# Two interleaved recurrences on one core: half of the second one's input product is issued behind the first one's reset product

## The chip, the cores and the metric

The kernel runs on one core of one Trainium2 chip. The metric is the device time of one execution in microseconds; of the kernel before there are three timed runs and one profiled execution. All arithmetic of the part that matters here is in float32.

## The reference, cut to what matters

The input `x` is 32 rows of 256 steps with 256 features, and four layers are added to it one after the other. The first is a GRU, the second a leaky gated recurrence over the result, the third is computed with cumulative sums over time, and the fourth is a two-matrix network whose weights are made per row from `cond_1024`.

```python
# layer 0, for t = 0 .. 255, h starts at zero
z = sigmoid(x_t @ W_z + h @ U_z + vz)
r = sigmoid(x_t @ W_r + h @ U_r + vr)
hh = tanh(x_t @ W + (r * h) @ U + vh)
h = (1 - z) * h + z * hh
# layer 1 on x1 = x + (all h), for the same t, h1 starts at cond_1024
gate = sigmoid(h1 @ Wh.T + x1_t @ Wz.T + b)
h1 = tanh(h1 * (1 - alpha) + gate * x1_t)
# x2 = x1 + (all h1); then layers 2 and 3 on x2
```

So each of the 256 steps of the GRU depends on the one before. Layer 1 is a second recurrence that needs only step s of the first, and can run one step behind it.

## The kernel before, in words

**The state.** Feature dimensions of 256 are cut into NC = 2 chunks of 128, which is the depth of one pass through TensorE. The state of a step stands transposed, `hT` with 128 features by 32 rows in each chunk, so that it is the stationary operand of the products; the 256 outputs are cut into Q = 4 quarters of 64, one in each group of 32 PSUM partitions. One `product` is therefore a loop over two chunks and four quarters, which is eight matmuls in the source. The trace has sixteen pairs of weight load and matmul for each such product: every float32 matmul stands there twice.

**One turn of the loop** (`for t in range(T + 1)`) does step t of the first recurrence and step s = t - 1 of the second. TensorE's order in a turn is written out by hand (the loop stands in a `manual_schedule` block, so every engine executes in the order of the source):

1. `product(p_0[t], ..., hT, w_urz)`: reset and update gates from `hT`. ACT takes the sigmoid `r` in two halves (by_halves, L657), then the update gate `z` (L707), then the tanh of the second recurrence (`h1T`, L686).
2. `due(products, t)`: one product of side work, from a table of due times. In most turns it is half of a gate product for layer 2 (`pg`, L93), in others a product for the weights of layer 3 (`pw`, L429 and L489). Some early turns have none; four turns near the end have two.
3. `product(p_1[s], ..., pairs1[s], w_1z)`: the second recurrence's product of x + h. `pairs1` was added up by POOL (L750). Its last matmul also waits for `z_done`, the update gate of this turn (`after(done, z_done)`).
4. DVE forms `rh = r * h` in two halves (L725) and transposes each (`rhT`, L649); then `product(p_0[t], ..., rhT, w_uh)`, the reset product.
5. `product(p_1[s], ..., h1T, w_1h)`: the second recurrence's product of its state. After it ACT can take its sigmoid `gt` (L755).
6. ACT takes the tanh of the candidate in two halves (`other`, L657), DVE scans `h` (L639) and transposes it to `hT` (L649). Meanwhile TensorE does `project(t + 1)`, the product of the next x with `W_rzh`, 192 columns wide. In two of every four turns `project` first starts a new PSUM tile of the first recurrence with four bias matmuls of 384 columns (`begin("0", ...)`, L600).
7. Every eighth turn, a new PSUM tile of the second recurrence is started behind the projection with four bias matmuls of 512 columns (`begin_1`, L600). It waits for `gt`, as `p_1` has one buffer.
8. ACT scales `h1T` into `pairs1` (L757), then any side sigmoid that is due (`gate_f` and `gate_i`, L130). DVE transposes `gt` (L766) and scans `pre` (L639), from which ACT takes `h1T` in the next turn.

After the loop come layers 2 and 3 (from 735 us on), which the diff does not touch.

Of the kernel before, what the change touches and what calls it, by code (L numbers as in the profile page):

```python
# [19 lines left out]
NC = D // P  # L20
# [19 lines left out]
def kernel(ctx: ExitStack, tc: tile.TileContext, a, out: bass.AP):  # L40
# [23 lines left out]
    def flat(x):  # L64
        return x.rearrange("p c b -> p (c b)")
# [114 lines left out]
    with ExitStack() as rec:  # L180
# [27 lines left out]
        def load_wq(name, g):  # L208
            w, src = weights(name, g)
            nc.sync.dma_start(out=w, in_=src)  # L210
            return w
# [3 lines left out]
        def load_x(i):  # L215
            xTs[i] = xp.tile([P, NC, TB, B], FP, name=f"xT_{i}", tag="xT")
            nc.sync.dma_start(out=xTs[i], in_=a["xT"][:, i])
# [24 lines left out]
        with tc.manual_schedule():  # L242
# [30 lines left out]
            w_1z = load_wq("l1_Wz", 1)  # L273
# [291 lines left out]
        def due(when, t):  # L565
            return [f(*args) for f, args in when.get(t, ())]

        def product(ps, cols, hT, w):


            for k in range(NC):
                for j in range(Q):
                    last = nc.tensor.matmul(  # L573
                        ps[j * B : (j + 1) * B, cols],
                        hT[:, k, :],
                        w[:, k, j, :],
                        start=False,
                        stop=False,
                        skip_group_check=True,
                        tile_position=(0, j * B),  # L580
                    )
            return last

        def after(later, earlier):

            tc.add_manual_dep(
                later.ins,
                earlier.ins.name,
                mybir.DependencyInfo(mybir.DependencyClass.Sync, mybir.DependencyReason.DATA),
                reason="a wait taken early",  # L590
            )
# [21 lines left out]
        def cols_0(t, first, last):  # L613
            at = t // 2 % U0 * 3 * S
            return slice(at + first * S, at + (last + 1) * S)

        def cols_1(s):
            u = s if s < U1_0 else (s - U1_0) % U1
            return slice(u * S, (u + 1) * S)

        def step_tile(name):
            return sp.tile([P, NC, B], FP, name=name, tag=name)
# [9 lines left out]
        def pair_tile(name, bufs=3):  # L632
            return sp.tile([P, S, 2], FP, name=name, tag=name, bufs=bufs)
# [11 lines left out]
        def turned(name, src):  # L645

            dst = step_tile(name)
            for c in range(NC):
                nc.vector.transpose(dst[:, c], src[:, bass.ts(c, B)])  # L649
            return dst  # L650

        def by_chunk(x):
            return x.rearrange("p (c b) -> p c b", b=B)

        def by_halves(dst, src, function):
            for c in range(NC):
                nc.scalar.activation(dst[:, bass.ts(c, B)], src[:, bass.ts(c, B)], function)  # L657

        def x_of(t):
            return xTs[t // TB][:, :, t % TB, :]  # L660

        p_0, p_1, pairs1, h1s = {}, {}, {}, {}

        def project(t):
            if t // 2 % U0 == 0:
                ps = begin("0", slice(0, 3 * S), U0, t)
                for u in range(U0):
                    p_0[t + 2 * u] = ps
            return product(p_0[t], cols_0(t, 0, 2), x_of(t), w_x)

        def begin_1(s, steps):
            ps = begin("1", slice(3 * S, 4 * S), steps, s)
            for u in range(steps):
                p_1[s + u] = ps

        with tc.manual_schedule():
            h1T = condT
            project(0)
            late = None

            def finish_1():

                nonlocal h1T
                s, pre = late
                h1T = h1s[s] = step_tile("h1T")
                nc.scalar.activation(flat(h1T), pre, AF.Tanh)  # L686

            def residual(s):
                return nc.gpsimd.tensor_add(  # L689
                    X2[:, :, :, s], by_chunk(pairs1.pop(s)[:, :, 0]), h1s.pop(s)  # L690
                )

            for t in range(T + 1):
                s, run0, run1 = t - 1, t < T, t >= 1
                due(transfers, t)
                if run0 and t % TB == 0 and t // TB + 2 < NB:
                    load_x(t // TB + 2)
                if run0:
                    keep = pair_tile("keep")
                    z, kept = keep[:, :, 0], keep[:, :, 1]  # L700
                    if t > 0:
                        rz_done = product(p_0[t], cols_0(t, 0, 1), hT, w_urz)
                        r = sp.tile([P, S], FP, name="r", tag="r")
                        by_halves(r, p_0[t][:, cols_0(t, 0, 0)], AF.Sigmoid)
                    else:
                        nc.gpsimd.memset(kept, 0.0)
                    z_done = nc.scalar.activation(z, p_0[t][:, cols_0(t, 1, 1)], AF.Sigmoid)  # L707
                if late is not None:
                    finish_1()
                    late = None  # L710
                due(moves, t)
                due(products, t)
                if run1:
                    if s == 0:
                        begin_1(0, U1_0)
                    done = product(p_1[s], cols_1(s), by_chunk(pairs1[s][:, :, 0]), w_1z)
                    if run0:

                        after(done, z_done)
                rh_done = kept_done = None  # L720
                if run0 and t > 0:
                    rh = sp.tile([P, S], FP, name="rh", tag="rh")
                    for c in range(NC):
                        cs = bass.ts(c, B)
                        rh_done = nc.vector.tensor_mul(rh[:, cs], r[:, cs], h[:, cs])  # L725
                    rhT = turned("rhT", rh)
                    product(p_0[t], cols_0(t, 2, 2), rhT, w_uh)

                    kept_done = nc.vector.scalar_tensor_tensor(
                        kept, z, 1.0, h, ALU.subtract, ALU.mult, reverse0=True  # L730
                    )

                    after(kept_done, rz_done)
                if t >= 3:
                    done = residual(t - 3)
                    if rh_done is not None:
                        after(done, rh_done)
                for done in due(additions, t):
                    if done is not None:
                        after(done, kept_done)  # L740
                due(sums, t)
                if run1:
                    product(p_1[s], cols_1(s), h1T, w_1h)
                if run0:
                    other = others[t % 2]
                    by_halves(other[:, :, 1], p_0[t][:, cols_0(t, 2, 2)], AF.Tanh)
                    h = multiply_add("h", other, keep, NC)
                    hT = turned("hT", h)
                    pairs1[t] = pair_tile("pairs1", 6)
                    nc.gpsimd.tensor_add(by_chunk(pairs1[t][:, :, 0]), x_of(t), hT)  # L750
                    if t + 1 < T:
                        project(t + 1)
                if run1:
                    gt = sp.tile([P, S], FP, name="gt", tag="gt")
                    nc.scalar.activation(gt, p_1[s][:, cols_1(s)], AF.Sigmoid)  # L755
                    for c in range(NC):
                        nc.scalar.activation(  # L757
                            by_chunk(pairs1[s][:, :, 1])[:, c], h1T[:, c], AF.Copy,
                            scale=leak[:, c : c + 1],
                        )  # L760
                    if t % U1 == U1_0 and run0:

                        begin_1(t, min(U1, T - t))
                    due(sigmoids, t)
                    other = others[2 + t % 2]
                    nc.vector.transpose(other[:, :, 1], gt)  # L766
                    late = s, multiply_add("pre", other, pairs1[s])
            for t in sorted(t for t in transfers if t > T):
                due(transfers, t)
            finish_1()  # L770
            for s in (T - 2, T - 1):
                residual(s)
# [242 lines left out]
```

## Time and profile before

| | |
|---|---|
| median of three runs | 955.35 us (955.17 to 957.66) |
| the profiled execution's own time | 956.46 us |
| its span, first to last instruction | 954.6 us |
| mean granted TensorE clock | 0.995 |
| TensorE busy | 919.4 us, 96% of the span |
| VectorE (DVE) busy | 788.4 us, 83% |
| ScalarE (ACT) busy | 572.3 us, 60% |
| GpSimd (POOL) busy | 236.5 us, 25% |

The recurrences take the first 735 us or so of the span. In the views, PE is the matmul stream and PEld the weight loads. A row of the timeline gives the start and the length in microseconds, the engine, the line, what is written from what, the shape, the number of like instructions merged into the row, and in square brackets how long the engine sat idle before it and what released it. A row of the waits gives engine, line, what was waited for, the total in microseconds, the number of times and the longest. Lines with L573 are the matmuls of all products, so they are told apart by their tiles: `w_U_rz` (step 1), `w_l_Wz` (step 3), `w_U_h` (step 4), `w_l_Wh` (step 5), `w_W_rzh` (step 6). Ends of matmuls are modelled: a matmul of 64 columns is drawn 219 ns long although the next group starts 56 ns after it.

### The profile page before, as it was taken

The numbers are of one execution on the slowest core, as the hardware profiler recorded it, in microseconds if no ns is written. First come the engines' busy times: TensorE is split into PE (matmuls) and PEld (weight loads), VectorE is DVE, ScalarE is ACT, GpSimd is POOL, SyncE is SP. The second block draws the span as 40 slices with busy tenths as digits, with TensorE's granted clock in tenths as the row PEclk, the third lists the DMA queues.
The fourth block names the chain that finished last, engine by engine and source line by source line (L and its number), as shares of the span: only waits on it lengthen the run. The fifth ranks groups of instructions, "written<-read, shape, count | busy, mean of one in ns | idle before, by whom it ended". The sixth has DMA issues, their size and how long they took to land.

```text
span 954.6 us, 55121 instructions
## 1 busy us (share of the span) xinstructions
PE 919.4 (96%) x22806; PEld 630.6 (66%) x22806; DVE 788.4 (83%) x3409; ACT 572.3 (60%) x2648; POOL 236.5 (25%) x594
## 2 busy tenths in 40 slices
PE   7999999999999999999999999999998989999978
PEld 4666666666666666666666666666675557777756
DVE  5767788888888888888888888888776799999994
ACT  3455555555555555555555555555554788889972
POOL 1233322222222222222222222222222022222222
PEclk9999999999999999999999999999999999999989
DMA  8344212222222222222222222432241457777543
GB/s 265 108 126 147 79 51 92 65 73 92 70 92 77 92 66 67 91 70 90 69 86 76 65 97 66 131 119 83 73 128 54 122 165 230 224 228 224 188 158 117
DMA packets 104158, 107.71 MB, mean 113 GB/s; under 512 B 9153, under 2 KB 86241, under 8 KB 103906
## 3 DMA queue, kind: packets, MB, share of 16 engines
q1 hardware_dynamic: 103906, 104.18, 34.4%
q8 instruction: 179, 2.93, 1.3%
q14 instruction: 73, 0.60, 0.2%
HBM read 59.06 MB, written 45.09 MB: 109 GB/s over the span
## 4 chain that ended last, share of the span: by engine, by line
PE 80%; DVE 13%; ACT 3%; issue 2%; DMA 1%; POOL 0%; DVEq 0%; POOLq 0%; ACTq 0%
PE p L573 45%; PE ps_l L889 10%; PE pg L93 10%; PE ps_c L93 5%; DVE h L639 5%; PE p L600 3%; PE ps_g L93 2%; PE pw L489 2%; ACT other L657 2%; DVE hT L649 1%; ACT r L657 1%; DVE rh L725 1%; DVE cc L848 1%; DVE gate_g L138 1%; PE pw L429 1%
## 5 line engine op out<-in xcount | busy, mean ns | idle before, releaser
L573 PE MATMUL p<-w_W_rzh,xT 128*32 128x192 f32 x4096 | 214.8, 326 | 0.2 <-issue 0.2
L657 ACT ACTIVATE other<-p 128x32 f32<-128x32 f32 x512 | 74.2, 199 | 172.9 <-PE p L573 172.9
L639 DVE TENSOR_TENSOR_SCAN h<-other,keep 128x64 f32<-128x64 f32 x512 | 121.3, 278 | 66.3 <-ACT other L657 62.7
L573 PE MATMUL p<-w_U_rz,hT 128*32 128x128 f32 x4080 | 165.4, 279 | 6.0 <-DVE hT L649 0.2
L750 POOL TENSOR_TENSOR pairs<-xT,hT 128x64 f32<-128x64 f32 x256 | 82.2, 321 | 326.9 <-DVE other L766 273.6
L657 ACT ACTIVATE r<-p 128x32 f32<-128x32 f32 x510 | 72.8, 195 | 149.0 <-PE p L573 149.0
L689 POOL TENSOR_TENSOR X<-pairs,h1T 128x64 f32<-128x64 f32 x256 | 103.0, 402 | 214.9 <-DVE rhT L649 211.8
L573 PEld LDWEIGHTS p<-w_U_rz,hT 128*32 128x32 f32 x4080 | 97.4, 108 | 84.3 <-DVE hT L649 83.4
L639 DVE TENSOR_TENSOR_SCAN pre<-other,pairs 128x128 f32<-128x128 f32 x256 | 123.3, 481 | 34.2 <-ACT pairs L757 0.7
L573 PEld LDWEIGHTS p<-w_W_rzh,xT 128*32 128x32 f32 x4096 | 124.9, 110 | 22.4 <-issue 1.9
L573 PEld LDWEIGHTS p<-w_l_Wz,pairs 128*32 128x32 f32 x4096 | 79.2, 110 | 86.0 <-issue 69.2
L757 ACT ACTIVATE pairs<-h1T,leak 128x32 f32<-128x32 f32 x510 | 133.6, 314 | 0.4
L573 PE MATMUL p<-w_l_Wz,pairs 128*32 128x64 f32 x4096 | 120.3, 225 | 5.1 <-ACT keep L707 1.6
L573 PE MATMUL p<-w_U_h,rhT 128*32 128x64 f32 x4080 | 106.6, 221 | 0.4 <-issue 0.4
L573 PE MATMUL p<-w_l_Wh,h1T 128*32 128x64 f32 x4080 | 104.7, 219 | 0.8 <-issue 0.7
L725 DVE TENSOR_TENSOR rh<-r,h 128x32 f32<-128x32 f32 x510 | 74.9, 188 | 32.1 <-ACT r L657 5.7
L649 DVE STREAM_TRANSPOSE hT<-h 128x32 f32<-128x32 f32 x512 | 84.1, 198 | 0.0
L882 POOL TENSOR_TENSOR X<-X,w 128x512 f32<-128x512 f32 x32 | 41.4, 1306 | 165.3 <-DVE w L875 76.8
L649 DVE STREAM_TRANSPOSE rhT<-rh 128x32 f32<-128x32 f32 x510 | 80.0, 195 | 0.0
L573 PEld LDWEIGHTS p<-w_l_Wh,h1T 128*32 128x32 f32 x4080 | 76.4, 110 | 1.3 <-issue 1.0
L573 PEld LDWEIGHTS p<-w_U_h,rhT 128*32 128x32 f32 x4080 | 69.7, 108 | 5.5 <-issue 0.6
L686 ACT ACTIVATE h1T<-pre 128x64 f32<-128x64 f32 x256 | 69.5, 271 | 1.4 <-DVE pre L639 1.4
(108 smaller groups left out, 1470.5 us busy)
## 6 DMA issues: line engine op xcount, KB each, us to landing
adapted<-wm SPq DMA_DIRECT2D x128, 128.0 KB
wt<-adapted SPq DMA_DIRECT2D x28, 512.0 KB
xT<-in_xT_dram SPq DMA_DIRECT2D x32, 256.0 KB
w<-in_W_dram SPq DMA_DIRECT2D x32, 256.0 KB
out_dram<-y SPq DMA_DIRECT2D x32, 256.0 KB
gates<-gate_i SPq DMA_DIRECT2D x48, 128.0 KB
gates<-gate_s SPq DMA_DIRECT2D x48, 128.0 KB
gates<-gate_g SPq DMA_DIRECT2D x48, 128.0 KB
```

The source lines that it names most:

```text
L93: nc.tensor.matmul(ps[:, 0 : (h1 - h0) * (rows.stop - rows.start) * CT].rearrange("p (h b t) -> p h b t", h=h1 - h0, t=CT), w[:, k, e * P ...
L573: last = nc.tensor.matmul(ps[j * B : (j + 1) * B, cols], hT[:, k, :], w[:, k, j, :], start=False, stop=False, skip_group_check=True, tile_ ...
L639: nc.vector.tensor_tensor_scan(*(x[:, ns].rearrange("p n u -> p (n u)") for x in (done, other, pairs)), 0.0, ALU.mult, ALU.add,)
L649: nc.vector.transpose(dst[:, c], src[:, bass.ts(c, B)])
L657: nc.scalar.activation(dst[:, bass.ts(c, B)], src[:, bass.ts(c, B)], function)
L686: nc.scalar.activation(flat(h1T), pre, AF.Tanh)
L689: return nc.gpsimd.tensor_add(X2[:, :, :, s], by_chunk(pairs1.pop(s)[:, :, 0]), h1s.pop(s))
L725: rh_done = nc.vector.tensor_mul(rh[:, cs], r[:, cs], h[:, cs])
L750: nc.gpsimd.tensor_add(by_chunk(pairs1[t][:, :, 0]), x_of(t), hT)
L757: nc.scalar.activation(by_chunk(pairs1[s][:, :, 1])[:, c], h1T[:, c], AF.Copy, scale=leak[:, c : c + 1],)
L882: after(nc.gpsimd.tensor_add(x, x, ws[g][:, b]), on_vector)
L889: nc.tensor.matmul(ps[:, e, :], matrices[row][:, m, k, e * P : (e + 1) * P], src[:, k, :], start=(k == 0), stop=(k == NC - 1),)
```

## The change

`product` gets a list of chunks. The second recurrence's product of x + h (step 3) does only its first chunk where the whole stood, and its second chunk behind the reset product (step 4), ahead of the product of `h1T` (step 5). The wait for `z_done` is now on the last matmul of the first chunk. The number of instructions on every engine is the same, and no other engine's instructions move.

```diff
-        def product(ps, cols, hT, w):
+        def product(ps, cols, hT, w, chunks=range(NC)):
-            for k in range(NC):
+            for k in chunks:
                 for j in range(Q):
                     last = nc.tensor.matmul(
...
-                    done = product(p_1[s], cols_1(s), by_chunk(pairs1[s][:, :, 0]), w_1z)
+                    x_and_h = p_1[s], cols_1(s), by_chunk(pairs1[s][:, :, 0]), w_1z
+                    done = product(*x_and_h, [0])
                     if run0:
 
                         after(done, z_done)
...
                 if run1:
+
+                    product(*x_and_h, [1])
                     product(p_1[s], cols_1(s), h1T, w_1h)
```

## The prediction

> **What bounds the kernel now.** The page comes first, and it misleads:
>
> ```profile
> PE 919.4 (96%) x22806; PEld 630.6 (66%) x22806; DVE 788.4 (83%) x3409; ACT 572.3 (60%) x2648; POOL 236.5 (25%) x594
> PE 80%; DVE 13%; ACT 3%; issue 2%; DMA 1%; POOL 0%; DVEq 0%; POOLq 0%; ACTq 0%
> ```
>
> TensorE looks like the bound, in busy time and in the chain that ended last. But matmul ends are modelled: every product is drawn 0.15 to 0.35 us longer than the stretch after which the next can start. So I went on to the waits, where the weight loads show what TensorE stands for:
>
> ```profile
> ACT other L657 <- PE p L573: 172.9, 255, 1.3
> ACT r L657 <- PE p L573: 149.0, 255, 1.4
> PEld p L573 <- DVE hT L649: 83.4, 249, 0.6
> DVE h L639 <- ACT other L657: 62.7, 154, 1.2
> ```
>
> In 249 of 255 turns TensorE stands idle for `hT`. For `rhT` no wait is listed, which would say that TensorE itself is late at the reset product; that is what this change would cure. The timeline of one turn, in narrow windows, decides:
>
> ```profile
> 402.58 0.27 PEld L573 LDWEIGHTS p<-w_l_Wz,pairs 128*32 128x32 f32 x16 [0.33 <-issue]
> 402.55 0.21 DVE L649 STREAM_TRANSPOSE rhT<-rh 128x32 f32<-128x32 f32 x1
> 402.68 0.18 DVE L649 STREAM_TRANSPOSE rhT<-rh 128x32 f32<-128x32 f32 x1
> 402.81 0.27 PEld L573 LDWEIGHTS p<-w_U_h,rhT 128*32 128x32 f32 x16
> ...
> 403.94 0.18 DVE L649 STREAM_TRANSPOSE hT<-h 128x32 f32<-128x32 f32 x1
> 404.17 0.38 PEld L573 LDWEIGHTS p<-w_U_rz,hT 128*32 128x32 f32 x16 [0.26 <-DVE hT L649]
> ```
>
> The first half of `hT` ends at 404.12, the load that needs it starts at 404.17; the first half of `rhT` ends at 402.76, its load starts at 402.81. Read one instruction at a time, both hand-overs take 53 ns. Over the trace, the first load of the reset product comes 52 to 54 ns behind its transpose in 249 of 255 turns, that of its second chunk 52 to 54 ns behind the second transpose in 245. So both halves of the loop are latency chains: hT, gate product, `r`, `rh`, `rhT` (1.435 us) and reset product, tanh, scan, `hT` (1.364 us), together 2.80 us a turn. The product of x + h ends barely in time, but in time.
>
> **Taken from in front of the reset product.** Eight of sixteen matmuls leave. In a stream, groups of four 64-column matmuls start 56 ns apart (the product of `h1T`, 16 matmuls, takes 223 ns to the start of the next), so 112 ns leave. Worth:
> - Turns without side work already have this state: there the x + h product is all issued 235 ns before the reset product, and they last 2796 ns on average. Turns with a gate product last 2798.5, turns with four `pw` matmuls for layer 3 2806. If the difference is TensorE's lateness, it all goes: 172 x 2.5 = 0.43 us and 32 x 10 = 0.33 us.
> - Four late turns with two side products last 2885 ns; there the reset product comes 115 ns behind `rhT`. 4 x 88 = 0.35 us.
> - In two turns (5 and 250) TensorE is hundreds of ns late after a stall of its own: between 0 and 112 ns each, 0.11 us for both.
>
> In all 1.2 us, not the 255 x 0.112 = 28.6 us that the busy share promises. The ends are 0.35 us and 1.3 us.
>
> **Put behind the reset product.** The same eight matmuls, 112 ns, now stand ahead of the product of `h1T`, the projection, the bias matmuls and so the next gate product. No bank, wait or semaphore is added; the last reset matmul carries its own count in the built program, and the tanh waits for that. What is queued behind is where the cost must be looked for. In a turn without bias matmuls TensorE then stands idle (0.43 us before that `w_U_rz` row, 0.26 to 0.27 us in the others), but idle weight loads are not a margin of the matmul stream. The stretch from the start of the last group to the gate product is:
>
> ```profile
> 403.94 0.40 PE L600 MATMUL p<-parts,eye 128*32 128x512 bf16 x4
> 404.18 0.65 PE L573 MATMUL p<-w_U_rz,hT 128*32 128x128 f32 x16
> ...
> 406.08 0.35 PE L600 MATMUL p<-parts,eye 128*32 128x384 bf16 x4
> 406.73 0.35 PE L573 MATMUL p<-w_W_rzh,xT 128*32 128x192 f32 x4
> 406.98 0.65 PE L573 MATMUL p<-w_U_rz,hT 128*32 128x128 f32 x16
> ```
>
> - A group of the gate product follows another 109 ns later, but the first after an idle stretch 133 ns: 24 ns of slack that a late TensorE gets back.
> - Turns that start a tile of the first recurrence (406.08): the last projection group starts 243 ns before the gate product and occupies 162 ns (the spacing of such groups). Margin 243 - 162 + 24 = 105 ns against 112. 119 such turns are 7 to 8 ns late: 0.95 us.
> - Turns that start a tile of the second (403.94): the 512-column group starts 242 ns ahead. Its own length in a stream is not shown; the 384-column one occupies 163 ns, so 217 in proportion. Margin 242 - 217 + 24 = 49 ns, 62 ns late. 30 turns: 1.86 us. If it occupied only the 162 of the projection: 8 ns and 0.2 us; with twice 163, 5 us. I take proportion, since the float32 version of the same matmul, in the one turn where it streams, takes 428 ns, twice 214.
> - The other 96 turns have a margin above 0.26 us: nothing.
> - Six disturbed turns (2, 3, 4, 19, 31, 248) start the gate product as soon as TensorE can: 0 to 112 ns each; half, 0.34 us.
> - `gt` comes 112 ns later, and behind it ACT's two scalings, a side sigmoid and DVE's `pre`. Cover: the scalings end at 401.38, `pre` starts at 401.73 behind DVE's own transpose that ends at 401.59, so 0.16 us beyond the hand-over. A side sigmoid (406.88 for 0.46) ends 0.21 us before the gate product that reuses its bank (407.55). `begin_1` waits for `gt`, ends near 403.76 before and near 403.87 after, while the projection keeps TensorE until 404.05. Without cover it would be 112 ns a turn.
>
> A lateness here is not given back: the chain that follows has no slack.
>
> **Sum.** +1.86 + 0.95 + 0.34 - 0.43 - 0.33 - 0.35 - 0.11 = +1.9 us. Against the profiled execution (956.46 us: 954.6 span, 1.9 around it) that is 958.4; that execution lies 1.1 us above the median, so against the median of 955.35 I predict 957.3. About 0.3% (2.9 us) is what a measurement of this kernel can tell from no change; this is 0.2%.
>
> A rule of the Trainium skill would give another sign. By the page "TensorE: Matmul & The Clock Gate", section "Back-to-back issue gap", matmuls of 1 to 64 columns follow each other after some 60 cycles, an issue floor of about 25 ns. An estimate from it makes the moved piece, two rounds, 50 ns instead of 112: both margins would cover it but for a nanosecond or so, and the sum would be about -0.9 us. The rows of this trace say 56 ns a round for float32, so the measurement is taken.
>
> **The rivals.**
> - *The thin margin (slower).* 149 turns pay every nanosecond by which the moved stretch exceeds its margin. At 118 ns instead of 112, or with the 24 ns of start-up slack not given back in full (18), the sum passes +2.9 us and the change is measurably slower; at 130 ns it is +4.6, near 960.0. For it: no row of before shows a reset product followed by this one, and the margin is 7 ns wide of the mark already. Against: the stream's spacing of 56 ns stays the same from product to product. Chance 0.39.
> - *TensorE is late at the reset product after all (faster).* If the 53 ns were TensorE's and not the hand-over's, every turn would gain up to 112 ns, and the time fall to 927. Against: the same 53 ns stands at `hT`, where TensorE is idle. A smaller way: some 20 turns lose 6 us in all to stalls of TensorE that have no releaser ("issue"); half gone is -3, near 954. Chance 0.08 for both.
> - *The change doesn't do what it says:* the tanh waiting for the second chunk too would cost 255 x 0.112, near 984. The program's order and counts speak against it; 0.02, on the slower side.
>
> **How the numbers follow.** My forecast, within 0.3%, 0.51; slower 0.41; faster 0.08. Own range of the forecast: gains of 0.35 to 1.3 against costs of 1.15 (the short end for 512 columns, none for the disturbed turns) to 3.5 (all of those) give -0.15 to +3.1 us; the far end of 5 us for 512 columns is left out. The runs before spread over 2.5 us, and the thin margin is held up to 130 ns: 955.0 to 960.0.
>
> **What would show it.** Right: the loads of the reset product still 53 ns behind `rhT`; the gate product 53 ns behind `hT` in its load, but its second group up to 8 ns late in the turns with 384-column bias matmuls and some 62 late in those with 512; `gt` 0.11 us later, `pre` not. Turns of 2796, about 2804 and about 2858 ns. Wrong: turns without bias matmuls that grow or shrink by more than 3 ns, a load of the reset product nearer than 53 ns, or `pre` waiting for ACT's scalings.

## The result, and the profile after

The changed kernel is slower by about the smallest step that can be measured: 960.57 us (median of eight runs, 959.55 to 963.66) against 956.46 us for the kernel before in the same comparison (eight runs, 955.17 to 958.81). The ratio is 1.0043 with an interval of 1.0031 to 1.0056. The forecast of 957.3 us and its range up to 960.0 both lie below it. The profiled execution took 960.90 us, its span is 959.0 us.

Busy time, the chain that ended last, and the waits of the changed kernel:

```profile
PE 927.4 (97%) x22806; PEld 643.0 (67%) x22806; DVE 788.1 (82%) x3409; ACT 591.2 (62%) x2648; POOL 236.1 (25%) x594
PE 92%; DVE 4%; DMA 1%; issue 1%; ACT 1%; SPq 0%; POOL 0%; DVEq 0%; ACTq 0%; POOLq 0%
```

```profile
ACT other L657 <- PE p L573: 170.1, 255, 0.9
ACT r L657 <- PE p L573: 124.6, 255, 1.4
...
DVE h L639 <- ACT other L657: 61.8, 154, 1.4
PEld p L573 <- DVE hT L649: 53.7, 239, 0.5
```

The instructions are as many as before. TensorE waits for `hT` in 239 turns, not in 249, and 53.7 us, not 83.4: some turns reach the gate product with little or no idle time in front of it. The chain now runs through TensorE for 92% where it was 80%. I read that as the same chain, followed through weight loads that no longer show a wait, and not as a measure of what the change cost.

The timeline of one turn, put together from narrow windows (start, length, engine, line):

```profile
405.02 0.21 DVE L649 STREAM_TRANSPOSE rhT<-rh 128x32 f32<-128x32 f32 x1
405.05 0.16 PEld L573 LDWEIGHTS p<-w_l_Wz,pairs 128*32 128x32 f32 x8 [0.33 <-issue]
405.28 0.27 PEld L573 LDWEIGHTS p<-w_U_h,rhT 128*32 128x32 f32 x16
405.48 0.18 PEld L573 LDWEIGHTS p<-w_l_Wz,pairs 128*32 128x32 f32 x8
405.59 0.30 PEld L573 LDWEIGHTS p<-w_l_Wh,h1T 128*32 128x32 f32 x16
...
406.41 0.19 DVE L649 STREAM_TRANSPOSE hT<-h 128x32 f32<-128x32 f32 x1
406.52 0.40 PE L600 MATMUL p<-parts,eye 128*32 128x512 bf16 x4
406.64 0.44 PEld L573 LDWEIGHTS p<-w_U_rz,hT 128*32 128x32 f32 x16 [0.15 <-DVE hT L649]
406.73 0.51 PE L573 MATMUL p<-w_U_rz,hT 128*32 128x128 f32 x12
```

The x + h product now stands as two rows of eight around the reset product. The reset product's first load still comes 53 ns behind the end of `rhT` (405.23 to 405.28), so nothing was gained in front of it. The gate product's first load also comes 53 ns behind `hT` (406.60 to 406.64, rounded), but its first matmul starts 88 ns after that load, because the 512-column group in front of it occupies TensorE until then; with no bias matmuls the gap is 2 ns.

### The profile page after: what moved, and what is told of

It is laid out like the page before. It is cut to its first block, busy times and chain, and to the rows that moved or that the text cites. A ratio compares the mean times of both kernels' runs of the same rounds, so it can differ in the third digit from the quotient of the medians.

```text
span 959.0 us, 55121 instructions
## 1 busy us (share of the span) xinstructions
PE 927.4 (97%) x22806; PEld 643.0 (67%) x22806; DVE 788.1 (82%) x3409; ACT 591.2 (62%) x2648; POOL 236.1 (25%) x594
## 4 chain that ended last, share of the span: by engine, by line
PE 92%; DVE 4%; DMA 1%; issue 1%; ACT 1%; SPq 0%; POOL 0%; DVEq 0%; ACTq 0%; POOLq 0%
PE p L573 56%; PE pg L93 12%; PE ps_l L892 10%; PE ps_c L93 5%; PE p L600 3%; PE ps_g L93 2%; PE pw L489 2%; DMA w_W_rzh<-in_W_rzh_dram 1%; DVE cc L851 1%; PE pg L115 1%; PE pw L429 1%; DMA in_i<-gates 1%; DVE w L857 1%; ACT r L657 1%; DVE w L869 0%
## 5 line engine op out<-in xcount | busy, mean ns | idle before, releaser
L573 PE MATMUL p<-w_l_Wz,pairs 128*32 128x64 f32 x4096 | 168.5, 225 | 7.2 <-ACT keep L707 5.8
L573 PE MATMUL p<-w_U_rz,hT 128*32 128x128 f32 x4080 | 162.7, 275 | 0.6 <-issue 0.5
L573 PEld LDWEIGHTS p<-w_l_Wz,pairs 128*32 128x32 f32 x4096 | 97.6, 110 | 90.2 <-issue 69.1
L573 PEld LDWEIGHTS p<-w_U_rz,hT 128*32 128x32 f32 x4080 | 100.7, 108 | 56.4 <-DVE hT L649 53.7
L573 PE MATMUL p<-w_U_h,rhT 128*32 128x64 f32 x4080 | 110.1, 225 | 0.0
```

Of the source, the lines that this page charges most:

```text
L573: last = nc.tensor.matmul(ps[j * B : (j + 1) * B, cols], hT[:, k, :], w[:, k, j, :], start=False, stop=False, skip_group_check=True, tile_ ...
```

## The experiments

Two numbers were taken from the trace of every run. A turn is the time from one gate product's first load to the next. **Eight turns** is the sum over the eight places (t mod 8) of the median turn length in turns 9 to 240, in ns: what the undisturbed loop costs. It occurs 31.75 times. **Stalls** is the sum, over turns 1 to 254, of all that a turn exceeds its place's median by, where that is over 15 ns, in us. Turns 1 to 6 are long in every kernel and make up 1.6 to 2.2 us of it (2.8 in e3); the late turns with two side products add up to at most 0.35 us where no stall falls on them. A profile is of one execution, which can lie at the edge of its kernel's times: those of e7 and after_2 (966.27 and 966.39 us) are the second slowest and the slowest of twelve, that of e11 (963.40 us) is the fastest of seven.

| run | time, us | ratio (95%) | eight turns, ns | stalls, us |
|---|---|---|---|---|
| before, first profile | 956.46 | | 22395 | 5.9 |
| after, first profile | 960.57 | 1.0043 (1.0031, 1.0056) | 22467 | 6.7 |
| e1_short_bias | 960.50 | 1.0010 (0.9991, 1.0030) | 22407 | 9.3 |
| e2_plain_turns | 959.02 | 1.0004 (0.9988, 1.0021) | 22374 | 8.4 |
| e3_whole_behind | 1011.47 | 1.0541 (1.0506, 1.0577) | 23690 | 21.7 |
| e4_before_again | 959.05 | 0.9997 (0.9981, 1.0014) | 22375 | 6.5 |
| e5_wide_turns | 962.30 | 1.0021 (1.0004, 1.0038) | 22459 | 7.9 |
| e6_narrow_turns | 960.55 | 0.9999 (0.9986, 1.0012) | 22421 | 8.1 |
| e7_after_again | 963.65 | 1.0032 (1.0017, 1.0048) | 22474 | 9.9 |
| e8_seven_behind | 991.55 | 1.0324 (1.0303, 1.0344) | 23045 | 20.0 |
| e9_front_only | 953.66 | 0.9941 (0.9921, 0.9961) | 22374 | 2.8 |
| e10_behind_only | 983.66 | 1.0260 (1.0237, 1.0284) | 22554 | 28.7 |
| e11_fewer_behind | 967.71 | 1.0091 (1.0072, 1.0109) | 22469 | 9.8 |
| e12_fewer_front | 955.18 | 0.9960 (0.9946, 0.9974) | 22393 | 3.2 |
| before_2, one execution | 956.22 | | 22376 | 5.6 |
| before_3, one execution | 961.55 | | 22398 | 7.7 |
| after_2 | 962.72 | 1.0038 (1.0023, 1.0052) | 22470 | 11.2 |
| after_3, one execution | 961.56 | | 22472 | 7.1 |

Times are medians where there is a ratio (the first profile of before has its own), and each ratio is to the kernel before on the same chip. That kernel's medians lie between 956.46 and 960.21 us, so times of different rows are compared by their ratios only. Edits are against the changed kernel unless said otherwise.

**Where the undisturbed time goes: which turns.** The second half is placed behind the reset product in some turns only.

```diff
+                    behind = CONDITION
-                    done = product(*x_and_h, [0])
+                    done = product(*x_and_h, [0] if behind else range(NC))
...
-                    product(*x_and_h, [1])
+                    if behind:
+                        product(*x_and_h, [1])
```

The condition is `t % 4 in (1, 2) and t % 8 != 2` (no bias matmuls follow), `t % 8 == 2` (the 512-column ones follow) and `t % 4 in (3, 0)` (the 384-column ones follow). In a fourth run the 512-column matmuls become 256-column ones, twice as often (`U0, U1 = 2, 4`), and the kernel before was run beside them.

> The second chunk goes behind the reset product only in the 96 turns that are followed by no bias matmuls; elsewhere the whole product of x + h stands in front as before. Theory A: no gate product is late (its second group at +135 ns in all classes of turns), undisturbed turns 2796 to 2800 ns, the time within 0.5 us of the kernel before. Theory B: part of the stalls comes with the moved piece wherever it lies, 96 of 254 turns of some 1.8 us, +0.7 us.

> The second chunk goes behind the reset product only in the 32 turns that are followed by the 512-column bias matmuls. Theory A: the second group of the gate product at +197 ns in the turns after these, +135 in all others; 62 ns per eight turns, +1.9 us. Theory B: next to nothing from so few turns, or a scatter without pattern.

> The second chunk goes behind only in the 126 turns that are followed by 384-column bias matmuls. Theory A: the second group of the gate product at +140 in those, +135 elsewhere; 4 x 5 = 20 ns per eight turns, +0.6 us, and up to 0.6 us more where a stall puts TensorE behind anyway: hardly to be told from none. Theory B: half of the moved pieces, so half of the unexplained 1.8 us.

> The changed kernel with U1 = 4 instead of 8: the bias matmuls that start a tile of the second recurrence are 256 columns wide and come every fourth turn, in turns that have no other bias matmuls. Theory A (the cost is the late gate product behind bias matmuls): the 256-column group should occupy about 109 ns, the margin is then 405 - 162 - 109 + 24 = 158 ns against 112, so the second group of the gate product stands at +135 ns behind its load again instead of +197 in the turns that follow; the time falls by 30 x 62 ns = 1.9 us against the changed kernel, to about 958.5 (some +2 us over the kernel before if 4.1 is the true difference). Theory B (the rest of the 4.1 us is more stalls of TensorE without a releaser, because the moved piece takes idle time in which instructions were supplied): the 62 ns vanish too, but the stalls inside the loop stay at 6.5 us or more.

> The kernel before itself, for a second profile and the scatter of the times: ratio 1.000 within 0.002. Theory A: stalls of TensorE without a releaser add up to anything from 4 to 8 us from run to run, as the 955.2 to 958.8 us of the timed runs would say, in both kernels alike. Theory B: they stay near 5.9 us here, with next to none between turns 60 and 240.

The ratios of e1, e2 and e6 can't be told from no change, but the turns can. The second group of the gate product starts this long after the first load (medians of turns 9 to 240, ns; plain turns are those with no bias matmuls):

| | no bias matmuls | behind 384 columns | behind 512 columns |
|---|---|---|---|
| before (four profiles) | 135 | 135 | 135 |
| after (four profiles) | 135 | 138 to 142 | 195 to 197 |
| e2, moved in plain turns | 135 | 135 | 135 |
| e5, moved before 512 columns | 135 | 135 | 195 |
| e6, moved before 384 columns | 135 | 142 | 135 |
| e1, 256 columns instead of 512 | 135 | 139 | 135 |

Each class of turns pays for itself alone: 60 to 62 ns behind the 512-column matmuls, 3 to 7 ns behind the 384-column ones, nothing elsewhere, and turning 512 columns into 256 takes the 62 ns away. In a 256-column turn of e1 the gate product's matmuls start with their loads:

```profile
405.61 0.29 PE L600 MATMUL p<-parts,eye 128*32 128x256 bf16 x4
405.74 0.64 PE L573 MATMUL p<-w_U_rz,hT 128*32 128x128 f32 x16
405.74 0.38 PEld L573 LDWEIGHTS p<-w_U_rz,hT 128*32 128x32 f32 x16 [0.15 <-DVE hT L649]
```

**A rival: the cut itself has a price.** If two halves cost something whatever is moved, a whole product behind the reset product would not cost twice the moved stretch less the margin.

```diff
-                    done = product(*x_and_h, [0])
-                    ... after(done, z_done)
...
-                    product(*x_and_h, [1])
+                    done = product(*x_and_h)
+                    if run0:
+                        after(done, z_done)
```

> The dose doubled: both chunks of the product of x + h, with the wait for the update gate, stand behind the reset product, 224 ns instead of 112. Theory A: turns with 384-column bias matmuls late by 5 + 112 = 117 ns (126 turns, 14.7 us), those with 512 columns by 62 + 112 = 174 ns (32 turns, 5.6 us), the other 96 not at all (margin 266 ns), less about 1 us of gains in front: +19 us, near 976, with the second group of the gate product at +250 and at +309 ns. gt comes 224 ns later, which passes the 0.16 us that DVE's pre has: if pre then delays rh, up to 64 ns a turn more, +16 us. If the cost were not the margin but a fixed price of cutting the product or of its place (theory C), it would stay near +4 us or, in proportion, +8.

The run cost far more than that, since its design was spoilt. With nothing left in front, the reset product's first load has to wait for a second engine:

```profile
437.79 0.21 DVE L649 STREAM_TRANSPOSE rhT<-rh 128x32 f32<-128x32 f32 x1
438.12 0.28 PEld L573 LDWEIGHTS p<-w_U_h,rhT 128*32 128x32 f32 x14 [0.62 <-ACT h1T L686]
```

It comes 116 ns behind `rhT` (438.00 to 438.12) in place of 53, and in the trace TensorE executes a semaphore instruction of 51 ns ahead of it. Plain turns grew from 2797 to 2880 ns by that alone. Above these 83 ns, turns with 384-column matmuls grew by 120 and those with 512 by 171 ns, which is 224 ns moved less the prediction's margins of 105 and 49 (119 and 175). To have it without the second wait, one quarter of the first chunk stays in front; a group of three quarters takes a round of TensorE like one of four, so 224 ns still move. `product` gets one more argument for it, the quarters of a chunk:

```diff
-                    done = product(*x_and_h, [0])
+                    done = product(*x_and_h, [0], lambda k: [Q - 1])
...
-                    product(*x_and_h, [1])
+                    product(*x_and_h, range(NC), lambda k: range(Q if k else Q - 1))
```

> The dose doubled without a second wait on the reset product, which spoilt the first attempt: seven of the eight matmuls of x + h stand behind the reset product, and one, with the wait for the update gate, stays in front. The piece behind is four groups of 56 ns, 224 ns. Theory A: the reset product's first load 53 ns behind rhT; the gate product's second group late by 117 ns after 384-column bias matmuls, by 174 after 512-column ones, not at all after none; eight turns add up to 22375 + 4 x 117 + 174 = 23017 ns, +20.4 us in the loop, a time near +21 us and more if stalls grow as in the first attempt (21.7 us). Theory C (a fixed price of the cut): +4 to +8 us.

> The changed kernel itself once more, for a second profile and a second set of times. Theory A (late gate products, 62 ns in 31 turns and 5 ns in some 120, and the rest of the first 4.1 us chance): turns by their place among eight add up to 22465 ns again, 70 to 90 more than in the kernel before, which is 2.3 to 2.9 us; the time is +2 to +4 us; the stalls without a releaser lie anywhere between 5 and 9 us, as they did in two profiles of the kernel before (5.9, 6.5) and two of variants (8.4, 9.3). Theory B (the moved piece lengthens the stalls): stalls above 7 us here and a time of +4 us or more.

Turns of e8 last 2800, 2918 and 2973 ns: nothing, 118 and 173 ns more with no, 384-column and 512-column bias matmuls. A fixed price of the cut would show in the plain turns and in the table above, and does not; margins of 105 and 49 ns and a stretch of 112 or 224 ns give all of these numbers. The second group of the gate product starts only 53 and 105 ns late in e8, not 117 and 174 as expected: the four quarters no longer run in step (in turn 131 the first starts 66 ns and more ahead of the other three). ACT's `r`, which needs all of them, starts 119 and 172 ns late. A 512-column turn of e8, in narrow windows:

```profile
421.87 0.89 PE L573 MATMUL p<-w_W_rzh,xT 128*32 128x192 f32 x16
422.02 0.34 DVE L649 STREAM_TRANSPOSE hT<-h 128x32 f32<-128x32 f32 x2
...
422.54 0.43 PE L600 MATMUL p<-parts,eye 128*32 128x512 bf16 x4
422.55 0.34 PEld L573 LDWEIGHTS p<-w_U_rz,hT 128*32 128x32 f32 x7
422.76 0.29 PE L573 MATMUL p<-w_U_rz,hT 128*32 128x128 f32 x3
```

There is no bracket on the gate product's load any more: `hT` has been there, and TensorE alone is late. The group of 512 columns occupies 216 ns (422.54 to 422.76). But the undisturbed turns of e8 explain only 20.9 us of its 31 (22386 to 23045 ns, 31.75 times); its stalls have grown from some 6 to 20 us. That was in no sum.

**The stalls.** They are idle time of TensorE in the middle of its stream, without a releaser. In the changed kernel, turn 31:

```profile
103.63 0.19 PEld L573 LDWEIGHTS p<-w_l_Wz,pairs 128*32 128x32 f32 x8
103.74 0.22 PEld L573 LDWEIGHTS p<-w_l_Wh,h1T 128*32 128x32 f32 x9
104.78 0.12 PEld L573 LDWEIGHTS p<-w_l_Wh,h1T 128*32 128x32 f32 x4 [0.82 <-issue]
```

Nine loads of one product are done, the tenth comes 0.82 us later, and all of them use the same `h1T`: nothing that the program waits for stands between. The clock is not it either: in all 18 profiles the granted TensorE clock is 1.00 through the whole loop, and half only before and behind it. To see what the stalls follow, the number of instructions was changed. In e9 the second half of the x + h product is left out; in e10 the whole product stands in front and the second chunk is added again behind, so it counts twice.

```diff
-                    product(*x_and_h, [1])
```

```diff
-                    done = product(*x_and_h, [0])
+                    done = product(*x_and_h)
```

> The front half of the change alone: the second chunk of x + h is left out and done nowhere, so the second recurrence gets half of that product. What the change takes from in front of the reset product, without what it puts behind. The prediction's gains were 1.2 us: 0.43 in turns with a gate product, 0.33 behind the four pw matmuls, 0.35 in the four late turns with two products, 0.11 in disturbed ones. The two profiles of the kernel before and of the kernel after say that the 0.43 was scatter between executions, and the 0.33 some 0.26. Theory A: -0.6 to -0.8 us (0.9993), with reset products 53 ns behind rhT and turns of 2796 to 2800 ns. Theory B (idle time of TensorE hides stalls): gate products behind as much idle as before, so stalls as before, 5 to 9 us, and fewer instructions to supply, so rather less.

> The other half alone: the whole product of x + h stands in front as before, and its second chunk is done once more behind the reset product, so that chunk counts twice. Theory A: the second group of the gate product at +140 and +197 ns, the four pw turns keep their 8 ns and the four late turns their 88; +2.6 to 3.0 us in undisturbed turns, up to 1 us in disturbed ones, in all +3 to +4 us (1.0031 to 1.0042). Theory B: the 16 added instructions a turn also have to be supplied; stalls clearly above 9 us and a time of +5 us or more.

The run e9 went beyond both expectations (5.7 us faster than the kernel before by its ratio, stalls of 2.8 us); e10 is what theory B forecast in kind, and far more of it. The queue that brings TensorE's instructions (packets, MB, share; its packets are of 16,384 bytes, and before's trace has 45,837 TensorE instructions to 179 of them, so 256 each), and two groups of weight loads (count, busy us and mean ns, idle us and its releasers), first of before, then of e9, then of e10:

```profile
q8 instruction: 179, 2.93, 1.3%
...
L573 PEld LDWEIGHTS p<-w_W_rzh,xT 128*32 128x32 f32 x4096 | 124.9, 110 | 22.4 <-issue 1.9 <-DMA w_W_rzh<-in_W_rzh_dram 0.5
...
L573 PEld LDWEIGHTS p<-w_l_Wh,h1T 128*32 128x32 f32 x4080 | 76.4, 110 | 1.3 <-issue 1.0 <-ACT h1T L686 0.3
```

```profile
q8 instruction: 163, 2.67, 1.3%
...
L573 PEld LDWEIGHTS p<-w_W_rzh,xT 128*32 128x32 f32 x4096 | 123.8, 110 | 22.1 <-issue 1.3 <-DMA w_W_rzh<-in_W_rzh_dram 0.2
...
L573 PEld LDWEIGHTS p<-w_l_Wh,h1T 128*32 128x32 f32 x4080 | 76.1, 110 | 0.4 <-ACT h1T L686 0.4
```

```profile
q8 instruction: 195, 3.19, 1.5%
...
L573 PEld LDWEIGHTS p<-w_W_rzh,xT 128*32 128x32 f32 x4096 | 130.1, 110 | 28.0 <-issue 9.1 <-DMA w_W_rzh<-in_W_rzh_dram 0.2
...
L573 PEld LDWEIGHTS p<-w_l_Wh,h1T 128*32 128x32 f32 x4080 | 78.8, 110 | 8.8 <-issue 8.3 <-ACT h1T L686 0.2
```

The share put down to "issue" grows from 1.3 to 1.9 to 9.1 us in the projection's loads, and from none to 1.0 to 8.3 us in those of `h1T`, which the edits do not touch. With nine in a hundred more packets the stalls are 29 us and not 6, with nine in a hundred fewer 3. But e9 and e10 change the amount as well as the place. The last pair keeps the matmuls: five of eight (three quarters of the first chunk are left out in both), in e11 with the second chunk behind the reset product, in e12 all in front.

```diff
 e11
-                    done = product(*x_and_h, [0])
+                    done = product(*x_and_h, [0], lambda k: [Q - 1])
...
                     product(*x_and_h, [1])
 e12
-                    done = product(*x_and_h, [0])
+                    done = product(*x_and_h, range(NC), lambda k: range(0 if k else Q - 1, Q))
...
-                    product(*x_and_h, [1])
```

> Three of the eight matmuls of x + h (three quarters of the first chunk) are left out, so TensorE has 12 instructions fewer a turn; of the five that stay, one is in front with the wait for the update gate, and the second chunk is behind the reset product as in the change. It is to be read against e12, which issues the same five in front. The run that left out four showed stalls of 2.8 us instead of 6 and was 5.6 us faster. Theory A (late gate products alone): the second group of the gate product at +140 and +197 ns, eight turns at 22450 to 22470 ns against 22375 to 22395, so e11 is 2.3 to 2.9 us slower than e12: near 0.997 against 0.994 of the kernel before. Theory B (part of the cost of the change is that idle time, which hid late instructions, is gone): with the supply relieved this part is small here too, so the same 2.3 to 2.9 us, less than the 3.1 to 4.1 us between the kernels after and before; were the difference 4 us here also, supply would have no part in it.

> The same five matmuls of x + h as in e11 (three quarters of the first chunk left out), all in front of the reset product. Theories A and B alike: no late gate product (+135 ns in all classes), stalls of 3 to 4 us, 4 to 5.6 us faster than the kernel before (0.994 to 0.996). If stalls do not fall with the number of TensorE's instructions, the time is that of the kernel before less 0.3 us.

> The kernel before, a third profile. Theory A (chance): stalls anywhere between 5 and 10 us, as in the kernel after. Theory B (placement lengthens the stalls): 5.5 to 7 us.

> The changed kernel, a third profile and a third set of times. Undisturbed turns: eight add up to some 75 ns more than in the kernel before, 2.4 us. Theory A: a ratio of 1.0025 within its interval, stalls as in the kernel before. Theory B: 1.0035 to 1.0045, stalls of 7 to 10 us.

> The kernel before, a fourth profile. Theory A (chance): stalls anywhere between 5 and 10 us. Theory B (placement): 5.5 to 7 us.

> The changed kernel, a fourth profile. Theory A (chance): stalls anywhere between 5 and 10 us. Theory B (placement): 7 to 10 us.

The loads of the projection, in e11 and in e12:

```profile
L573 PEld LDWEIGHTS p<-w_W_rzh,xT 128*32 128x32 f32 x4096 | 127.0, 110 | 25.5 <-issue 5.4 <-DMA w_W_rzh<-in_W_rzh_dram 0.8
```

```profile
L573 PEld LDWEIGHTS p<-w_W_rzh,xT 128*32 128x32 f32 x4096 | 125.1, 110 | 23.2 <-issue 3.0
```

The run e12 came out as expected, e11 did not: theories A and B both put it 2.3 to 2.9 us behind e12, and the ratios differ by 1.3%, or 12.5 us. In the profiles the loop of e11 takes 9.1 us longer than that of e12 (723.1 against 714.0). The undisturbed turns are 76 ns per eight longer, 2.4 us; the stalls are 9.8 against 3.2 us, which is the other 6.6. So the place lengthens them with the same matmuls. Two things are not equal in this pair: TensorE executes 100 more semaphore instructions of 51 ns in e11 (42,865 instructions in all against 42,765), and e11 has waits for ACT of 14.8 us in 37 turns, by tiles 36 of them at the x + h matmul that stayed in front; 19 of these turns are no longer than their place's median.

The number of instructions alone does not set the stalls: e11 has 12 matmuls and weight loads fewer a turn than the changed kernel and stalls as long, and e3 and e8 stall for 20 us and more with the kernel before's matmuls.

**Where in the stream the stalls stand.** The traces say more than the expectations asked. Number TensorE's instructions in the order of the program, each weight load followed by its matmul, with the semaphore instructions between. In turns 9 to 240 of the 18 profiles there are 190 idle times of over 150 ns between two weight loads of the same product where nothing is waited for. Counted from 0 and divided by 256, the load that ends them has the remainder 193 or 194 in all 190, the same place in all kernels, whatever their instructions a turn. One packet holds 256 instructions, so this is where TensorE enters a new packet. In 2,785 such entries the first load never starts less than 1.15 us behind the end of its packet, and 188 of the 190 stalls end within 1.8 us of it. The stall shown above is one of them: the packet ends at 103.44 us, the load starts at 104.78. So the stalls are instructions that come late.

How often a packet is entered close behind its end follows the stalls from kernel to kernel (packets counted in the trace, turns 9 to 240 in the last column):

| | packets | stalls, us | entered under 1.5 us behind the packet's end |
|---|---|---|---|
| e9 | 163 | 2.8 | 2 of 141 |
| e12, in front | 167 | 3.2 | 8 of 144 |
| before (four profiles) | 179 | 5.6 to 7.7 | 11 to 21 of 156 |
| after (four profiles) | 179 | 6.7 to 11.2 | 19 to 26 of 156 |
| e11, behind | 167 | 9.8 | 36 of 145 |
| e8 | 179 | 20.0 | 48 of 156 |
| e3 | 179 | 21.7 | 47 of 156 |
| e10 | 195 | 28.7 | 72 of 170 |

In the kernel pair itself it is less sure. Four profiles of before have stalls of 5.9, 6.5, 5.6 and 7.7 us, four of after 6.7, 9.9, 11.2 and 7.1. The means are 2.3 us apart, the ranges overlap, and two of the four executions of after are among the slowest of theirs, so 2.3 us may be too much.

## Why the prediction was wrong

The late gate products were foreseen, and their size too. What failed is the sum around them: the term of the disturbed turns, 0.34 us, which took the stalls as given, a gain of 0.43 us that is not there, and a base 1.1 us too low. The measured 960.57 us lies 0.6 us above the range's upper end.

**What the measured difference consists of.** Undisturbed turns: the mean of four profiles is 22386 ns before and 22471 after, so 85 ns times 31.75, or 2.7 us. The three ratios (1.0043, 1.0032, 1.0038) average 0.38%, or 3.6 us. About 1 us is left, and by the ratios' intervals anything between none and 2.5 us. The growth of the stalls would fill it; that they grow in this pair is not shown beyond chance. The forecast had 2.05 us for the undisturbed turns (1.86 + 0.95 - 0.43 - 0.33) and -0.12 us for all others (0.34 - 0.35 - 0.11).

**Right, by the steps.** Nothing was to be had in front of the reset product in the normal turn: 53 to 55 ns behind `rhT` (medians) in all runs but e3. The moved piece takes 112 ns: two groups 56 ns apart, as in the trace of before, and twice that in e8. The 512-column group was taken as 217 ns, measured 216; the gate product was to be 62 ns late behind it, measured 60 to 62. Behind the 384-column ones 7 to 8 ns was forecast, 3 to 7 measured. Plain turns are unchanged. `gt` hides its 0.11 us: `pre` waits for ACT 1.4 us in all, 0.7 before. The rule that the prediction cites from "Back-to-back issue gap" in the Trainium skill's page "TensorE: Matmul & The Clock Gate" is a floor of about 25 ns for one matmul of up to 64 columns. Taken for a round of four float32 matmuls, as the prediction's estimate has it, it would have made the change a gain; the 56 ns a round measured here decides against that.

**Right in part: the four late turns with two products.** In the first profile of before three of them last 2884 to 2887 ns and the fourth 3352, not all 2885. Behind the change the first (turn 242) lasts 2795, as forecast, but the second only falls to 2867; the other two are lengthened by stalls to 3051 and 3189. In e9, where the second chunk stands nowhere, three of the four last 2794 to 2805.

**Wrong: the gain of 0.43 us.** The step that read 2.5 ns from 172 gate-product turns took the difference of two means from one profile, 2798.5 less 2796. The same turns have means of 2796.3, 2796.7 and 2798.7 ns in the three further profiles of before, with no change made, and 2797.0 in e9, where the piece in front is gone. So no gain is to be seen beyond the scatter between executions. Without it, the forecast of the undisturbed turns is 2.5 us, near the 2.7 us. The other small gain was there: in the 32 turns with a `pw` product the stretch from the reset product to the next gate product fell from 1370 to 1373 ns to 1363 to 1365.

**Wrong: the term of the disturbed turns.** It took six turns from one profile, at 0 to 112 ns each, half of it, 0.34 us. It treated a stall as something that has happened already, behind which 112 ns more may or may not be late. The runs show that the stalls themselves move with what stands where: 3.2 and 9.8 us in e12 and e11 with the same matmuls, 20 us in e8, 2.8 and 28.7 us with fewer and more. They stand where TensorE enters a packet of instructions, and the prediction had no term for when packets come. In the pair the term was about 1 us by the ratios and 2.3 us by the profiles.

**Wrong: the base.** The sum was set on the median of three runs, 955.35 us; eight runs of the same comparison gave 956.46. That is 1.1 us of the 3.3 by which the forecast missed. The profiled execution, which the sum was made against first, happens to have the same 956.46 us; against it the forecast would have been 958.4, still 2.2 us short.

**The rivals.** The thin margin named the right side and the wrong mechanism: the stretch was 112 ns, the slack was given back, and no turn paid for a mis-sized margin. TensorE's lateness at the reset product is refuted by the 53 ns that stayed; half the stalls gone, by stalls that did not shrink. The tanh does not wait for the second chunk: no plain turn grew.

**What stays open** is why packets come late more often in one order than in another. That late instructions are what TensorE stands for is read from where the stalls stand; no run delayed the instructions by themselves. In the two longest stalls of the changed kernel behind turn 6 (turns 31 and 224) the packets start 5.85 and 5.88 us apart, where the median is some 4.2. The Trainium skill, page "Runtime: NRT & Kernel Launch", section "Instruction fetch mechanics", says that each engine's instructions are streamed in 16 KiB blocks of 256 instructions by a DMA queue of its own, and that this is mostly hidden. The 179 packets of 16,384 bytes in this trace agree with the first; the 28.7 us of stalls in e10 are not hidden. Why, with the same matmuls, the second chunk behind the reset product brings more late packets than in front (36 of 145 in e11, 8 of 144 in e12) no run shows.

## What to carry to other kernels

Work that is moved on an engine is priced by the margin at its new place, and for matmuls that margin is counted in spacings of the stream, not in idle time of weight loads: spacing, start-up slack and margin from one trace gave the new turn lengths to a few nanoseconds. Differences of two or three nanoseconds between classes of turns need a second profile before they become a gain, and the base should be as many runs as there are. Where "issue" appears in the middle of a product, number the engine's instructions and see whether the stalls stand at one place of 256, as they do here. Then fewer instructions can be worth more than their order: the loop without four matmuls of the source a turn (e9, which leaves half a product out) gained 5.7 us, and no order with all of them was measurably faster than the kernel before.

## What the hardware showed that was not expected

- TensorE stalls in the middle of a product with nothing to wait for, always where it enters a packet of 256 instructions: 190 of 190 idle times of over 150 ns in 18 profiles. With the long turns 1 to 6 they add up to 2.8 us in e9 and to 28.7 us in e10.
- The first load of a packet never started less than 1.15 us behind the packet's end (2,785 entries); the median was 2.0 to 2.2 us in the kernel before, 2.65 in e9 and 1.55 in e10.
- A second engine to wait for costs the first load of a product 63 ns: 116 instead of 53 ns behind the transpose in e3, with a semaphore instruction of 51 ns ahead of it.
- After an idle stretch the second group of the gate product comes 135 ns after the load in place of 109 in the stream, and a TensorE that is up to that much late gets these 24 to 26 ns back.
- Four bf16 matmuls side by side occupy 163 ns with 384 columns and 216 ns with 512, so in proportion to their columns.
